# Layer 1's mask: turned 32 by 32 on VectorE, spread over rows by one 512-column product, with degrees summed by runs

## The chip, the cores and the metric

The kernel runs on one core of one Trainium2 chip. The metric is the device time of one execution in microseconds (us). Five engines work side by side, each through its own queue in order: TensorE (PE, with the loads of its stationary operand shown apart as PEld), VectorE (DVE), ScalarE (ACT), GpSimd (POOL) and SyncE (SP), which here only issues DMA transfers. They wait for one another through semaphores.

## The reference, cut to what matters

Two layers work on 128 graphs of 128 nodes with 256 features. Layer 0 (layernorm, a convolution, message passing, a gated update) fills most of the time and is not changed. Layer 1 runs a two-layer graph convolution on five groups of the first 25 nodes and adds the fused result:

```python
GROUPS = [list(range(25)), [0..8], [0, 9..14], [6, 7, 8, 12, 13, 14], [3, 4, 5, 9, 10, 11]]
A = adj + jnp.eye(n)                       # of one group: adj_g = adj[:, idx][:, :, idx]
deg = jnp.sum(A, axis=-1)
dinv = jnp.where(deg == 0, 0.0, deg_safe ** (-0.5))
norm_adj = dinv[:, :, None] * A * dinv[:, None, :]
out = relu(einsum(norm_adj, x @ W) + b)    # twice, W1 then W2
fused = fused.at[:, idx, :].add(norm_w[g] * out_g)
```

What changes is how `norm_adj` is built. For each group it is the group's part of the adjacency matrix plus the identity, scaled by the inverse roots of the row sums.

## The kernel before

**Tiling of layer 1.** The groups together have 25 + 9 + 7 + 6 + 6 = 53 rows (`NR`), padded to `RP = 64`. Two graphs share the 128 partitions, `s * 64 + r` being row r of graph s. A block is 16 graphs (`SB`), so 8 pairs; there are 8 blocks. Each group's node list is cut into runs of consecutive nodes by `_runs()`: 1 + 1 + 2 + 2 + 2 = 8 runs (row offset r, first node n, width w).

**Constants.** `_constants()` builds one array that is loaded in two parts. Of its columns `et` (node n to row k of both halves), `same` (rows of one group), `diag`, `e4`, `ones2`, `sgrp` (which group a row belongs to, per half) and `ident` matter here.

**`prepare(blk)`, lines 1015 to 1079,** makes the scaled masks `ac` and the copies `r4` of one block, in steps parted by `yield`:
1. L1023: SP issues four loads of the 25x25 corners of 16 adjacency matrices into `aj`, nodes on 25 partitions, 16 graphs along the free axis.
2. L1029: POOL adds the identity and copies the 8 runs' columns into `b1`, 25 partitions by 16 graphs by 64 rows.
3. L1036: DVE sums `b1` by group into `dg`, 5 reductions.
4. L1042: PE makes `pa`, eight products, one for each pair: `b1` of the pair (128 columns) is stationary, `et` (64 columns) moves. L1044: DVE multiplies by `same` into `ac`. L1047: PE spreads `dg` over rows (`et` stationary, 80 columns move). L1050 to L1059: DVE and POOL pick the row's group and form the inverse root `dm`.
5. L1063 to L1065: DVE scales; L1068: PE; L1069: DVE; L1073: PE makes `pr4` (512 columns); L1077: DVE copies it to `r4`.

`block(blk)` then uses `ac` and `r4`: products `py` (L1093), the five groups' two layers in `first` (L1110) and `second` (L1119), then `turn`, `gather` and `fuse`.

**What sets the order.** All engines' programs are written out by a list scheduler, `Order.run`, at build time. Each part of the work is a generator; `yield cost, delay` says how much PE time the step just issued takes, and how long its next step should wait. Lanes share PE by weight. In the last call the lane `second` holds `setup_1` and then `prepare` and `block` of each block in turn, two of them open at once, at weight 0.2, beside layer 0's groups (`stage_c`), its loads, `fetch` and `rows`. Costs and delays change the order of all engines' instructions, but no instruction waits for a time: at run time an engine stops only at semaphores. `block(blk)` starts when `prepare(blk)` has ended and block `blk - 1` has passed its `gather` steps; `prepare(blk)` starts after `prepare(blk - 1)`. In layer 0's last stage the DMA issues on POOL (L837, L938, L954, L955) and the powers on POOL (L1007) stand in the same queue as `prepare`'s adds.

**Buffers.** `aj` and `dd` share one buffer (tag `dd`); `b1` is set to zero once in `setup_1`.

Of the kernel before, what the change touches and what calls it, by code (L numbers as in the profile page):

```python
# [9 lines left out]
FP = mybir.dt.float32  # L10
AF = mybir.ActivationFunctionType
ALU = mybir.AluOpType
# [7 lines left out]
P = 128  # L20
GB = 4
# [9 lines left out]
SB = 16  # L31
# [4 lines left out]
NG = len(GROUPS)  # L36
# [8 lines left out]
def _runs():  # L45

    out = []
    for g, nodes in enumerate(GROUPS):
        i = 0
        while i < len(nodes):  # L50
            j = i
            while j + 1 < len(nodes) and nodes[j + 1] == nodes[j] + 1:
                j += 1
            out.append((OFFS[g] + i, nodes[i], j - i + 1))
            i = j + 1
    return out
# [36 lines left out]
def _constants():  # L93

    row_node = [n for g in GROUPS for n in g]
    row_group = [i for i, g in enumerate(GROUPS) for _ in g]
    fwd, inv, tap = _fourier()
    parts = {
        "ident": np.eye(P),
        "mhalf": np.full((P, 8), -0.5),  # L100
        "fwd": fwd, "tap": tap, "inv": inv,
        "ones2": np.kron(np.eye(2), np.ones((RP, RP))),
        "et": np.zeros((P, 2 * RP)),
        "same": np.zeros((P, RP)),
        "diag": np.zeros((P, RP)),
        "e4": np.zeros((P, P)),
        "s2": np.zeros((P, 2 * WIDE)),
        "grp": np.zeros((P, NG)),
        "sgrp": np.zeros((P, 2 * NG)),
        "grpt": np.zeros((P, P)),  # L110
        "sel": np.zeros((P, P)),
        "emb": np.zeros((P, 12)),
    }

    roles = {0: [(2, 2, 0), (0, 0, 1), (1, 1, 0), (0, 0, 1)],
             1: [(0, 0, -1), (0, 0, 1), (1, 1, 0), (1, 1, 0)],
             2: [(1, 1, 0), (1, 1, 0), (0, 0, -1), (0, 0, 1)]}
    for j in range(GB):
        for role, factors in roles.items():
            for ch in range(3):  # L120
                k = WIDE * j + 3 * role + ch
                parts["sel"][ch, k] = 1
                parts["emb"][k] = np.array(factors).T.reshape(-1)
    for r, (n, g) in enumerate(zip(row_node, row_group)):
        for s in range(2):
            k = s * RP + r
            parts["et"][n, k] = 1
            parts["same"][k, [i for i in range(NR) if row_group[i] == g]] = 1
            parts["diag"][k, r] = 1
            for j in (2 * s, 2 * s + 1):  # L130
                parts["e4"][k, j * WIDE + n] = 1
            parts["s2"][k, s * WIDE + n] = 1
            parts["grp"][k, g] = 1
            parts["sgrp"][k, s * NG + g] = 1
            parts["grpt"][g, k] = 1
    at, o = {}, 0
    for name, a in parts.items():
        at[name] = (o, o + a.shape[1])
        o += a.shape[1]
    return np.concatenate(list(parts.values()), 1).astype(np.float32), at  # L140
# [67 lines left out]
def kernel(ctx: ExitStack, tc: tile.TileContext, x, adj, consts, vecs, w_se, conv1_w,  # L208
# [25 lines left out]
    def c(name):  # L234
        a, b = CAT[name]
        return cst[:, a:b]
# [725 lines left out]
    def setup_1():  # L962
        while len(E_DONE) < NQ:
            yield 0.0, 1.0
        near.close()
        pool = S["pool"] = ctx.enter_context(
            tc.tile_pool(name="l1", bufs=1, reuse_waits="tile"))
        S["pool2"] = ctx.enter_context(
            tc.tile_pool(name="l2", bufs=2, reuse_waits="tile"))
        b2s = pool.tile([NG, D], FP, tag="dd", name="b2s")  # L970
        nc.sync.dma_start(out=b2s, in_=b2)
        for n in range(2):
            load_w1(n)
        S["w2"] = weight(pool, W2, [P, 5, 4, D], "g (k p) o -> p g k o", "w2", nc.sync)
        S["ac"] = [pool.tile([P, SB // 2, RP], FP, name=f"ac{i}") for i in range(2)]
        r4 = S["r4"] = [pool.tile([P, QS, GB, NR], FP, name=f"r4{i}") for i in range(2)]
        S["yz"] = pool.tile([P, 2, SB, RP], FP, name="yz")
        S["b1"] = pool.tile([NN, SB, RP], FP, name="b1")
        for t in (*r4, S["yz"][:, 0], S["yz"][:, 1], S["b1"]):
            nc.gpsimd.memset(t, 0.0)  # L980
            yield 0.0, 4.0
        b2row = S["b2row"] = pool.tile([P, D], FP, name="b2row")
        pb2 = ptmp.tile([P, 512], FP, tag="tmp", name="pb2")
        nc.tensor.matmul(pb2[:, :D], c("grpt")[:NG], b2s, start=True, stop=True)
        nc.vector.tensor_copy(b2row, pb2[:, :D])
        P_DONE.add(-1)
        B1_DONE.add(-1)
        yield 0.5, 0.0
# [26 lines left out]
    def prepare(blk):  # L1015

        while not (blk - 1 in P_DONE and blk - 2 in {-2, *B1_DONE}):
            yield 0.0, 1.0
        pool, pool2, b1 = S["pool"], S["pool2"], S["b1"]
        ac, r4 = S["ac"][blk % 2], S["r4"][blk % 2]  # L1020
        aj = pool.tile([NN, SB, NN], FP, tag="dd", name=f"aj{blk}")
        for i in range(GB):
            nc.sync.dma_start(out=aj[:, i % 2 * 2 + i // 2::GB],  # L1023
                              in_=adj[blk * SB + i:(blk + 1) * SB:GB, :NN, :NN]
                              .rearrange("b n m -> n b m"))
        yield 0.0, 13.0 if blk < NBLK - 1 else 6.0

        for r, n, w in _runs():
            nc.gpsimd.tensor_tensor(b1[:, :, r:r + w], aj[:, :, n:n + w],  # L1029
                                    ident[:NN, None, n:n + w].to_broadcast([NN, SB, w]),  # L1030
                                    ALU.add)
        yield 0.0, 5.0

        dg = pool2.tile([NN, SB, NG], FP, tag="dg", name=f"dg{blk}")
        for g in range(NG):
            nc.vector.reduce_sum(dg[:, :, g], b1[:, :, OFFS[g]:OFFS[g] + SIZES[g]],  # L1036
                                 axis=mybir.AxisListType.X)
        yield 0.0, 7.0

        pa = ptmp.tile([P, SB // 2, RP], FP, tag="tmp", name=f"pa{blk}")  # L1040
        for p in range(SB // 2):
            nc.tensor.matmul(pa[:, p], b1[:, 2 * p:2 * p + 2, :].rearrange("n s r -> n (s r)"),  # L1042
                             c("et")[:NN, :RP], start=True, stop=True)
        nc.vector.tensor_mul(ac, pa, c("same")[:, None, :].to_broadcast([P, SB // 2, RP]))  # L1044

        pdg = ptmp.tile([P, SB // 2, 2, NG], FP, tag="tmp", name=f"pdg{blk}")
        nc.tensor.matmul(pdg.rearrange("p a s g -> p (a s g)"), c("et")[:NN],  # L1047
                         dg.rearrange("n b g -> n (b g)"), start=True, stop=True)
        dsel = pool.tile([P, SB // 2, 2 * NG], FP, tag="dsel", name=f"dsel{blk}")
        nc.vector.tensor_mul(dsel, pdg.rearrange("p a s g -> p a (s g)"),  # L1050
                             c("sgrp")[:, None, :].to_broadcast([P, SB // 2, 2 * NG]))
        dm = pool.tile([P, SB // 2], FP, tag="dm", name=f"dm{blk}")
        zo = pool.tile([P, SB // 2], FP, tag="zo", name=f"zo{blk}")
        nc.vector.reduce_sum(dm, dsel, axis=mybir.AxisListType.X)
        nc.vector.tensor_scalar(zo, dm, 0.0, None, op0=ALU.is_equal)
        nc.vector.tensor_add(dm, zo, dm)
        nc.gpsimd.tensor_tensor(dm, dm, c("mhalf"), ALU.pow)
        nc.gpsimd.tensor_mul(zo, zo, dm)
        nc.gpsimd.tensor_sub(dm, dm, zo)  # L1059
        yield 2.0, 7.0  # L1060

        dd = pool.tile([P, SB // 2, RP], FP, tag="dd", name=f"dd{blk}")
        nc.vector.tensor_mul(dd, c("diag")[:, None, :].to_broadcast([P, SB // 2, RP]),  # L1063
                             dm[:, :, None].to_broadcast([P, SB // 2, RP]))
        nc.vector.tensor_mul(ac, ac, dm[:, :, None].to_broadcast([P, SB // 2, RP]))  # L1065
        yield 0.0, 6.0
        pg = ptmp.tile([P, SB // 2, RP], FP, tag="tmp", name=f"pg{blk}")
        nc.tensor.matmul(pg, c("ones2"), dd, start=True, stop=True)  # L1068
        nc.vector.tensor_mul(ac, ac, pg)  # L1069
        yield 0.9, 3.0  # L1070

        pr4 = ptmp.tile([P, QS, 2, RP], FP, tag="tmp", name=f"pr4{blk}")
        nc.tensor.matmul(pr4.rearrange("p q a r -> p (q a) r"), c("e4"), ac,  # L1073
                         start=True, stop=True)
        for j in range(GB):
            s = slice(j * WIDE, (j + 1) * WIDE)
            nc.vector.tensor_copy(r4[s, :, j % 2 * 2 + j // 2, :], pr4[s, :, j % 2, :NR])  # L1077
        yield 0.9, 1.0
        P_DONE.add(blk)
# [174 lines left out]
```

## Time and profile before

| | |
|---|---|
| median of 3 runs | 2012.26 us (2009.02 to 2017.96) |
| the profiled execution | 2009.44 us |
| its span on the core | 2007.7 us |
| PE busy | 1960.1 us (98%), 12598 matmul records |
| DVE busy | 1352.3 us (67%) |
| ACT, POOL busy | 683.4 us (34%), 655.7 us (33%) |
| L1042, the eight products, all blocks | 128 records, 15.9 us busy |
| L1029, the adds on POOL | 64 instructions, 27.7 us busy |
| L1036, the reductions on DVE | 40 instructions, 10.1 us busy |

An fp32 product shows as two records. A record's busy time includes its passage through the pipeline and overlaps the next one's; how long a product holds PE is read from one start to the next. In rows of groups the columns are line, engine, operation, output and inputs, shapes, count, then busy time and mean duration in ns, then the engine's idle time just before and what ended it.

### The profile page before, as it was taken

How to read it: one execution, taken by the hardware profiler on the slowest of the kernel's cores; microseconds unless marked ns; L12 is line 12 of the kernel's file. 1: busy time of each engine (PE TensorE's matmuls, PEld its weight loads, DVE VectorE, ACT ScalarE, POOL GpSimd, SP SyncE). 2: the span in 40 equal slices, each digit the busy share in tenths (PEclk: the TensorE clock that was granted, in tenths of full speed). 3: DMA queues.
4: the chain of work that ended last, by engine and by line, in shares of the span. 5: the costliest groups of instructions: out<-in, count | busy, mean ns of one | idle time of the engine just before them, and what ended most of it. 6: DMA issues, size and time to landing. Idle time of an engine off the chain costs nothing.

```text
span 2007.7 us, 33356 instructions
## 1 busy us (share of the span) xinstructions
PE 1960.1 (98%) x12598; PEld 1625.4 (81%) x12598; DVE 1352.3 (67%) x3002; ACT 683.4 (34%) x1547; POOL 655.7 (33%) x897
## 2 busy tenths in 40 slices
PE   7999999999999999999999999999999999999998
PEld 5667888889888888878778878888888888888865
DVE  6775445885433576885885787778668867886652
ACT  4664222454222344222323232232323332322233
POOL 3452666332656111241331232222221322222320
PEclk9999999999999999999999999999999999999999
DMA  9997879744887743542433342443442433433331
GB/s 212 296 273 250 274 250 289 220 148 158 269 258 254 198 124 107 163 103 82 119 90 108 106 113 77 118 112 88 118 121 80 126 102 98 107 102 108 65 94 53
DMA packets 184106, 302.88 MB, mean 151 GB/s; under 512 B 28501, under 2 KB 131994, under 8 KB 183690
## 3 DMA queue, kind: packets, MB, share of 16 engines
q1 hardware_dynamic: 138762, 168.81, 28.9%
q0 software_dynamic: 44800, 131.66, 22.6%
q8 instruction: 100, 1.64, 0.3%
q14 instruction: 60, 0.49, 0.1%
q10 hardware_dynamic: 384, 0.28, 0.1%
HBM read 204.12 MB, written 109.05 MB: 156 GB/s over the span
## 4 chain that ended last, share of the span: by engine, by line
PE 87%; DVE 7%; DMA 3%; issue 1%; ACT 1%; SPq 1%; POOL 0%; DVEq 0%; ACTq 0%; POOLq 0%
PE p L755 41%; PE pa L531 7%; PE ph L1110 5%; PE pz L1119 5%; PE pm L642 5%; PE pc L422 4%; PE pb L531 3%; PE px L668 3%; PE pf L433 3%; PE pi L712 3%; PE pw L477 1%; PE py L1093 1%; PE ph L411 1%; DMA xa<-in_x 1%; PE pse L626 1%
## 5 line engine op out<-in xcount | busy, mean ns | idle before, releaser
L938 POOL DMA_DIRECT2D x1d<-xt x128 | 101.1, 815 | 467.2 <-DVE xt L936 454.9
L837 POOL DMA_DIRECT2D xt<-in_x x128 | 100.2, 789 | 173.8 <-DMA x1d<-xt 166.8
L563 DVE SCALAR_TENSOR_TENSOR y<-pa,kk 128x512 f32<-128x512 f32 x78 | 53.8, 690 | 151.2 <-ACT kk L562 151.1
L531 PE MATMUL pa<-wf,X 128*128 128x256 f32 x640 | 152.2, 381 | 0.0
L755 PE MATMUL p<-th,wrz 128*128 128x256 f32 x512 | 134.5, 385 | 0.0
L755 PE MATMUL p<-tc,wrz 128*128 128x256 f32 x512 | 131.4, 379 | 0.0
L755 PE MATMUL p<-tm,wrz 128*128 128x256 f32 x512 | 131.4, 379 | 0.0
L531 PEld LDWEIGHTS pa<-wf,X 128*128 128x128 f32 x640 | 118.1, 190 | 16.2 <-issue 2.0
L422 PE MATMUL pc<-c1w,hTa 128*128 128x256 f32 x512 | 121.2, 383 | 2.7 <-DVE X L439 1.5
L642 PE MATMUL pm<-wmsg,hT 128*128 128x256 f32 x512 | 121.5, 382 | 0.0
L1110 PE MATMUL ph<-yz,w 128*128 128x96 f32 (+3 forms) x640 | 109.3, 325 | 1.4 <-DVE yz L1095 1.4
L422 PEld LDWEIGHTS pc<-c1w,hTa 128*128 128x128 f32 x512 | 94.0, 191 | 19.9 <-DVE h L425 4.8
L755 PEld LDWEIGHTS p<-th,wrz 128*128 128x128 f32 x512 | 94.7, 190 | 19.1 <-issue 7.3
L1112 ACT ACTIVATE hh<-ph,vec 128x96 f32<-128x96 f32 (+3 forms) x160 | 63.6, 401 | 133.5 <-PE ph L1110 125.1
L724 ACT ACTIVATE xc<-xc,t_bn 128x256 f32<-128x256 f32 x128 | 58.2, 500 | 148.5 <-DVE xc L721 148.5
L755 PEld LDWEIGHTS p<-tc,wrz 128*128 128x128 f32 x512 | 97.3, 190 | 13.9 <-issue 0.8
L642 PEld LDWEIGHTS pm<-wmsg,hT 128*128 128x128 f32 x512 | 95.8, 190 | 15.2 <-ACT kk L562 1.4
L1119 PE MATMUL pz<-hh,w 128*128 128x96 f32 (+3 forms) x640 | 107.5, 322 | 0.7 <-DVE yz L1121 0.7
L755 PEld LDWEIGHTS p<-tm,wrz 128*128 128x128 f32 x512 | 97.3, 190 | 13.2
L1110 PEld LDWEIGHTS ph<-yz,w 128*128 128x128 f32 x640 | 88.3, 193 | 22.4 <-issue 15.6
L1119 PEld LDWEIGHTS pz<-hh,w 128*128 128x128 f32 x640 | 86.3, 191 | 18.6 <-DVE yz L1121 1.3
L755 PE MATMUL p<-hTc,wrz 128*128 128x256 f32 x384 | 99.3, 381 | 1.2 <-DVE z L829 1.2
(204 smaller groups left out, 4464.8 us busy)
## 6 DMA issues: line engine op xcount, KB each, us to landing
wf<-wfd SPq DMA_DIRECT2D x160, 256.0 KB
wfd<-ws POOLq DMA_DIRECT2D x64, 320.0 KB, 10.2
yd<-y POOLq DMA_DIRECT2D x80, 256.0 KB, 4.0
yt<-yd SPq DMA_DIRECT2D x64, 320.0 KB
w<-in_W SPq DMA_DIRECT2D x40, 512.0 KB
xa<-in_x SPq DMA_DIRECT2D x128, 128.0 KB
hTd<-hTa POOLq DMA_DIRECT2D x32, 512.0 KB, 6.6
hT<-hTd SPq DMA_DIRECT2D x32, 512.0 KB
```

Of the source, the lines that this page charges most:

```text
L422: nc.tensor.matmul(pc[:, i], hT[:, k, (2 * h + i) * N:(2 * h + i + 1) * N], c1w[:, k], start=(k == 0), stop=(k == 1))
L433: nc.tensor.matmul(pf[:, i, :F * NB], h1[:, 2 * h + i, k * P:(k + 1) * P], fwd, start=True, stop=True)
L531: nc.tensor.matmul(ps, xk(k), WF[f][:, k, s], start=(k == 0), stop=(k == 1))
L642: nc.tensor.matmul(pm[:, i], hT[:, k, j * N:(j + 1) * N], LATE["wmsg"][:, k], start=(k == 0), stop=(k == 1))
L668: nc.tensor.matmul(px[:, dc, i], msgs[h][:, i, dc * P:(dc + 1) * P], aT[:, 2 * h + i], start=True, stop=True)
L712: nc.tensor.matmul(pi[w * WIDE:(w + 1) * WIDE, :, :, n].rearrange("p k g c -> p g k c"), inv[:F, o:o + WIDE], yt[:, n // 2::2].rearrange(" ...
L755: nc.tensor.matmul(ps[:, m], w[:, i, k, m * P:(m + 1) * P], factor(i, x, t), start=first and j == 0, stop=last and j == len(n) - 1, skip_g ...
L837: nc.gpsimd.dma_start(out=xt[a * WIDE:(a + 1) * WIDE].rearrange("p b d c -> p (b d) c"), in_=slices(x[q * GB:(q + 1) * GB])[a])
L938: nc.gpsimd.dma_start(out=slices(x1d[q])[a], in_=xt[a * WIDE:(a + 1) * WIDE].rearrange("p b d c -> p (b d) c"))
L1110: nc.tensor.matmul(ph, w1[:, k, m * P:(m + 1) * P], yz[:, k, :, o:o + n], start=(k == 0), stop=(k == 1))
L1112: nc.scalar.activation(hh[:, m], ph, AF.Relu, bias=v("b1", g * 4 + m))
L1119: nc.tensor.matmul(pz, w2[:, g, m, cc * P:(cc + 1) * P], hs[g][:, m], start=(m == 0), stop=(m == 3))
```

## The change

The load puts the two graphs of a pair on two blocks of 32 partitions (`s * 32 + n`), 8 pairs along the free axis, each padded to 32 columns; `aj` has a buffer of its own, set to zero once in `setup_1`. DVE transposes `aj` in 32x32 blocks into `at`, 64x256. POOL adds the identity (a new constant, `eye`) and copies the 8 runs from `at` into `b1`, now 64 partitions by 8 pairs by 64 rows. DVE sums `aj`, without the identity, by run into `dg`, 8 reductions, and 1 is added to the degree later. One product replaces the eight: `et`, now with 64 rows, is stationary, and all of `b1` (512 columns) moves. The degree product moves 64 columns in place of 80. Adds and reductions stand in one step with a delay of 9.0 in place of two with 5.0 and 7.0; the PE cost of the next step is 1.1 in place of 2.0. `setup_1` has one more memset.

```diff
@@ constants
-        "sgrp": np.zeros((P, 2 * NG)),
+        "sgrp": np.zeros((P, len(_runs()))),
+        "eye": np.zeros((P, WIDE)),
...
-            parts["et"][n, k] = 1
+            parts["et"][s * WIDE + n, k] = 1
+            parts["eye"][s * WIDE + n, n] = 1
...
-            parts["sgrp"][k, s * NG + g] = 1
+            parts["sgrp"][k, [i for i, (o, _, _) in enumerate(_runs())
+                              if OFFS[g] <= o < OFFS[g] + SIZES[g]]] = 1
@@ setup_1
-        S["b1"] = pool.tile([NN, SB, RP], FP, name="b1")
-        for t in (*r4, S["yz"][:, 0], S["yz"][:, 1], S["b1"]):
+        S["b1"] = pool.tile([2 * WIDE, SB // 2, RP], FP, name="b1")
+        S["aj"] = pool.tile([2 * WIDE, SB // 2, WIDE], FP, name="aj")
+        for t in (*r4, S["yz"][:, 0], S["yz"][:, 1], S["b1"], S["aj"]):
             nc.gpsimd.memset(t, 0.0)
             yield 0.0, 4.0
@@ prepare
-        aj = pool.tile([NN, SB, NN], FP, tag="dd", name=f"aj{blk}")
+        aj = S["aj"]
         for i in range(GB):
-            nc.sync.dma_start(out=aj[:, i % 2 * 2 + i // 2::GB],
+            s = i // 2 * WIDE
+            nc.sync.dma_start(out=aj[s:s + NN, i % 2::2, :NN],
                               in_=adj[blk * SB + i:(blk + 1) * SB:GB, :NN, :NN]
                               .rearrange("b n m -> n b m"))
         yield 0.0, 13.0 if blk < NBLK - 1 else 6.0
 
-        for r, n, w in _runs():
-            nc.gpsimd.tensor_tensor(b1[:, :, r:r + w], aj[:, :, n:n + w],
-                                    ident[:NN, None, n:n + w].to_broadcast([NN, SB, w]),
-                                    ALU.add)
-        yield 0.0, 5.0
-
-        dg = pool2.tile([NN, SB, NG], FP, tag="dg", name=f"dg{blk}")
-        for g in range(NG):
-            nc.vector.reduce_sum(dg[:, :, g], b1[:, :, OFFS[g]:OFFS[g] + SIZES[g]],
-                                 axis=mybir.AxisListType.X)
-        yield 0.0, 7.0
+        at = pool.tile([2 * WIDE, SB // 2, WIDE], FP, tag="dd", name=f"at{blk}")
+        nc.vector.transpose(at.rearrange("p a n -> p (a n)"), aj.rearrange("p a n -> p (a n)"))
+        dg = pool2.tile([2 * WIDE, SB // 2, len(_runs())], FP, tag="dg", name=f"dg{blk}")
+        for i, (r, n, w) in enumerate(_runs()):
+            nc.gpsimd.tensor_tensor(b1[:, :, r:r + w], at[:, :, n:n + w],
+                                    c("eye")[:2 * WIDE, None, n:n + w]
+                                    .to_broadcast([2 * WIDE, SB // 2, w]), ALU.add)
+            nc.vector.reduce_sum(dg[:, :, i], aj[:, :, n:n + w], axis=mybir.AxisListType.X)
+        yield 0.0, 9.0
 
-        for p in range(SB // 2):
-            nc.tensor.matmul(pa[:, p], b1[:, 2 * p:2 * p + 2, :].rearrange("n s r -> n (s r)"),
-                             c("et")[:NN, :RP], start=True, stop=True)
+        nc.tensor.matmul(pa, c("et")[:2 * WIDE], b1, start=True, stop=True)
...
-        pdg = ptmp.tile([P, SB // 2, 2, NG], FP, tag="tmp", name=f"pdg{blk}")
-        nc.tensor.matmul(pdg.rearrange("p a s g -> p (a s g)"), c("et")[:NN],
-                         dg.rearrange("n b g -> n (b g)"), start=True, stop=True)
+        pdg = ptmp.tile([P, SB // 2, len(_runs())], FP, tag="tmp", name=f"pdg{blk}")
+        nc.tensor.matmul(pdg, c("et")[:2 * WIDE], dg, start=True, stop=True)
...
         nc.vector.reduce_sum(dm, dsel, axis=mybir.AxisListType.X)
+        nc.vector.tensor_scalar(dm, dm, 1.0, None, op0=ALU.add)
...
-        yield 2.0, 7.0
+        yield 1.1, 7.0
```

More of the change, by code (lines that the diff above doesn't have):

```diff
@@ L1047, in prepare @@
-        nc.tensor.matmul(pdg.rearrange("p a s g -> p (a s g)"), c("et")[:NN],
-                         dg.rearrange("n b g -> n (b g)"), start=True, stop=True)
-        dsel = pool.tile([P, SB // 2, 2 * NG], FP, tag="dsel", name=f"dsel{blk}")
-        nc.vector.tensor_mul(dsel, pdg.rearrange("p a s g -> p a (s g)"),
-                             c("sgrp")[:, None, :].to_broadcast([P, SB // 2, 2 * NG]))
+        pdg = ptmp.tile([P, SB // 2, len(_runs())], FP, tag="tmp", name=f"pdg{blk}")
+        nc.tensor.matmul(pdg, c("et")[:2 * WIDE], dg, start=True, stop=True)
@@ L1052, in prepare @@
+        dsel = pool.tile([P, SB // 2, len(_runs())], FP, tag="dsel", name=f"dsel{blk}")
+        nc.vector.tensor_mul(dsel, pdg, c("sgrp")[:, None, :].to_broadcast(
+            [P, SB // 2, len(_runs())]))
         dm = pool.tile([P, SB // 2], FP, tag="dm", name=f"dm{blk}")
```

## The prediction

> **What bounds the kernel now.** I read the page's busy times first, then the busy times by stage, then the one row of timeline where the changed lines run, and last the waits of TensorE (PE).
>
> ```profile
> PE 1960.1 (98%) x12598; PEld 1625.4 (81%) x12598; DVE 1352.3 (67%) x3002; ACT 683.4 (34%) x1547; POOL 655.7 (33%) x897
> ...
> PE 87%; DVE 7%; DMA 3%; issue 1%; ACT 1%; SPq 1%; POOL 0%; DVEq 0%; ACTq 0%; POOLq 0%
> ```
>
> PE is busy 98% of the span and carries 87% of the chain that ended last. Busy shares of a pipelined PE are generous, so I look at the stages in which the changed code runs: PE has instructions of layer 1 from 838 us on. In each row the columns are stretch, its length, and busy time (with instructions) of PE, weight loads, DVE, ACT, POOL.
>
> ```profile
> 838.00:900.00 62.00, 59.96 (x377) 49.60 (x377) 53.60 (x117) 16.53 (x35) 22.04 (x33) 0.97 0.36 89
> 1000.00:1200.00 200.00, 196.64 (x1253) 163.17 (x1252) 150.67 (x325) 56.96 (x126) 54.26 (x76) 1.00 0.38 104
> 1400.00:1600.00 200.00, 200.00 (x1327) 166.40 (x1326) 154.89 (x331) 59.70 (x130) 53.72 (x77) 1.00 0.39 108
> 1916.00:2008.00 92.00, 78.21 (x516) 57.50 (x516) 36.49 (x94) 29.47 (x68) 15.58 (x26) 0.98 0.27 74
> ```
>
> Seven of the eight `prepare` calls end their PE work inside 838 to 1916, where PE is full and DVE has a quarter free; the eighth falls in the tail, where 13.8 us of PE are idle. In a full stage PE time removed is time gained, one for one, and other engines' work is free as long as it is not late. The row of the timeline around the first call (start, length, engine):
>
> ```profile
> 871.24 0.59 PE L755 MATMUL p<-xc,wn 128*128 128x256 f32 x2
> 871.76 1.99 PE L1042 MATMUL pa<-cst,b 25*128 25x64 f32 x16
> 873.60 0.40 PE L1047 MATMUL pdg<-dg,cst 25*128 25x80 f32 x2
> 873.92 1.23 PE L755 MATMUL p<-hTc,wrz 128*128 128x256 f32 x4
> ```
>
> Lengths overlap (a matmul's end is modelled), so I use starts. An fp32 product is two records: 8 products of 64 columns are 16 records and hold PE from 871.76 to 873.60, 1.84 us; the degree product holds it to 873.92, 0.32 us. The starts in the trace give 1.83 and 0.33 us in all eight blocks. What a 512-column product holds PE for stands in the same trace, twice per block:
>
> ```profile
> 1905.80 1.02 PE L1068 MATMUL pg<-dd,cst 128*128 128x512 f32 x2
> 1906.66 0.59 PE L755 MATMUL p<-xm,wn 128*128 128x256 f32 x2
> ```
>
> That is 0.86 us, the figure of 12 of the 16 products L1068 and L1073; two have 0.96 and two, in the tail, 1.06.
>
> **What the Trainium skill says.** "TensorE: Matmul & The Clock Gate", LDWEIGHTS: a load takes its stationary columns / 1.2 in ns, whatever the rows, so 106.7 ns for 128 columns. The trace agrees: 16 records in 1.83 us are 114 ns each, although only 64 columns move. So the old form pays for sixteen weight loads and not for its columns, and 64 instead of 25 stationary rows should cost nothing. The same page, Back-to-back issue gap, calls a wide matmul bound by its moving columns; here the two records of 512 fp32 columns took 0.86 us, twice the 0.43 of the two of 256 just ahead of them (1905.37 to 1905.80). "VectorE: DVE Perf Modes", errata section, prices an fp32 tensor_tensor at (N+151)/0.96 ns. The trace is near it for the reductions too: 400 elements took 551 ns (574 by the formula). "GPSIMD Engine Reference", Performance versus the Vector engine: about 2.6 cycles per element for two inputs. The trace agrees: from the groups below 2.0 ns per element (2.4 cycles at the page's 1.2 GHz) plus 238 ns an instruction, and 743 ns for 256 elements in 128 partitions (L525; 745 by that line), so partitions are free and only the elements in each count.
>
> The groups of adds and reductions, kept apart by shape (busy us, mean ns):
>
> ```profile
> L1029 POOL TENSOR_TENSOR b<-aj,cst 25x400 f32<-25x400 f32 x8 | 8.3, 1032 | 0.1
> L1029 POOL TENSOR_TENSOR b<-aj,cst 25x16 f32<-25x16 f32 x8 | 2.2, 270 | 0.0
> ...
> L1036 DVE TENSOR_REDUCE dg<-b 25x16 f32<-25x400 f32 x8 | 4.4, 551 | 0.0
> L1036 DVE TENSOR_REDUCE dg<-b 25x16 f32<-25x96 f32 x16 | 3.2, 236 | 0.0
> ```
>
> **The change part by part,** per `prepare` call, eight of them.
>
> *PE.* Removed: the eight products, 1.83 us. Added: one product of 512 columns, 0.86 us. The degree product goes from 80 to 64 moving columns and from 25 to 64 rows; it is two loads of 128 columns either way, so 0.33 us stays. Net 1.83 - 0.86 = 0.97 us, times 8 = 7.8 us. With the slower 0.96 it is 7.0; if the degree product's first load now hides under the 512 columns (one load, 0.11 us, saved) it is 8.6.
>
> *POOL.* Before, 8 adds over 16 graphs: 8 x 238 ns + 16 x 53 elements x 2.0 ns = 3.6 us. After, 8 adds over 8 slots, 424 elements: 1.9 + 0.8 = 2.7 us. POOL is freed by 0.9 us. But its first add now waits for the DVE transpose; behind it on POOL stand the DMA issues of L837, L938, L954/955 and the powers of L1007.
>
> *DVE.* Five reductions over 848 elements become eight over 424. By their groups 137 ns + 1.04 ns per element, so 1.57 us before and 1.54 after. Added: one `tensor_scalar` of 8 elements (0.17, as L1055) and the transpose of 64x256. No row shows that size; a 128x512 transpose took 709 ns (L719) and 1052 with a permuting pattern (L929), so half, 0.35 to 0.53 us; I take 0.4. Together +0.55 us. Against this DVE's idle time for `pa` shrinks: it stood 1.50 us ahead of 873.79 until the eighth product was out, and should stand some 1.0 us less. DVE is not the bound (about 151 of 200 us busy), so nothing reaches the end. With its cover gone, 0.55 x 8 = 4.4 us is the most.
>
> *The DMA.* Four loads as before, 400 packets of 100 bytes, to other partitions. They now meet DVE, not POOL, first. In the trace the packets of every block are over within 6.4 us of the first issue, and the adds, whose step the transpose takes, start 14 to 49 us after the last issue. So no wait. `aj` no longer shares a buffer with `dd`; only its own old readers hold it, long done. The late constants grow by 30 columns, 15 KB on 461.5, under layer 0; the extra memset (64x256; 25x1024 took 0.97 us) is some 0.25 us of POOL, once.
>
> *The order.* One pause of 9 us replaces 5 and 7, the PE cost goes from 2.0 to 1.1, and the setup has one more memset with a pause of 4 us. The first block's chain starts 4 us later and is 3 + 0.9 us shorter: nothing, under a PE busy 59.96 of 62 us. From then on the list scheduler picks other interleavings. Where PE is at 200 of 200 us there is little to win; between 900 and 1916 it idles 5.4 us in all.
>
> *The tail.* Here the chain of `prepare(7)` is exposed:
>
> ```profile
> 1961.06 1.12 PE L1073 MATMUL pr<-ac,cst 128*128 128x512 f32 x2
> 1962.11 0.65 PE L1163 MATMUL pfu<-zt,s2w 128*64 128x256 f32 x4
> 1963.91 3.10 PE L1093 MATMUL py<-r,x1h 128*128 128x212 f32 x16 [1.15 <-DVE r L1077]
> ```
>
> Block 7's first product waits 1.15 us for the copies of the last step of `prepare(7)`. `prepare`'s product stands after the third `second` of block 6; with 9 for 5 + 7 it comes one or two steps of 1.95 us earlier, and so does all behind it: 2 to 4 us, more than the 1.15 and the 0.17 ahead of `pg`. I count 1.3 us, with bounds 0 and 3.
>
> Sum: 7.8 + 1.3 = 9.1 us. The profiled execution took 2009.44 us (span 2007.7, 1.7 around it): 2000.3. The median of the runs, 2012.26, lies 2.8 above that execution, so on the median **2003**.
>
> **The rivals.**
>
> *A better order.* The new order also fills PE gaps that the change does not touch: 5.4 us between 900 and 1916, 2.0 between 838 and 900, 3.7 in the waits from 1916 to 1926. Half of these is some 6 us: 15 us in all, 1997. For it: the rows show the gaps. Against: nothing in the change aims at them.
>
> *The gain is eaten.* The 512-column product exposes its first load and a wait (1.06 as in the tail, 0.3 of issue more), or the order opens gaps as it closes others. Gain 0.97 - 0.5 = 0.5 per block and nothing in the tail: 4 us, 2008. For it: PE's weight loads of L755 already stand 20.3 us in gaps put down to issue from 838 us on.
>
> *Late masks, slower.* Before, the DMA, POOL and DVE took turns with 5 + 7 us between them; now DMA, DVE, POOL, PE have 9. The chain needs 0.4 (transpose) + 2.7 (adds) = 3.1 us, a little more with its semaphores, and the reductions run beside it. It decides when DVE lags PE's place in the order by over some 6 us: every microsecond more stops PE in each block. A lag of 9 us costs 3 x 8 = 24 us, less the 9.1: about 2027. Against: DVE used PE's results within 1 to 2 us around 852 to 872 (L882 at 871.87, right behind its product at 871.24), and the adds started 12.8 to 46 us ahead of PE's product in all blocks, so some 10 us with the pause cut by 3.
>
> **How the numbers follow.** A change of 0.5%, 10 us, is about what a measurement of this kernel can tell from none; runs of the same kernel spread by 9 us. Likeliest case 0.56 (2000 to 2007), better order 0.20, eaten 0.14, late 0.10. The bound of 0.5% faster is 2002.2. Of the likeliest case I put a bit under four tenths below it, with all of the better order: 0.22 + 0.20 = 0.42 faster. The rest of it and the eaten case: 0.34 + 0.14 = 0.48 same. Late: 0.10 slower. The range takes in the eaten case down to no gain at all, and leaves out the late case and the far end of the better order: 1995 to 2012.
>
> **What would show it.** Right: two records at the new product with 0.86 us to the next start, no PE wait at it; DVE waits under 1 us for `pa`; eight adds in about 2.7 us; PE busy time down by 7 to 9 us; no wait of `py` for the copies of L1077's successor in the tail. Wrong: DVE idle before the transpose with the DMA as releaser, PE idle before the new product with POOL as releaser, or new PE waits at L755.

## The result and the profile after

The changed kernel took 1999.99 us (median of 6 runs, 1997.61 to 2005.25), the kernel before 2012.4 in the same comparison: ratio 0.9935, 95% interval 0.9914 to 0.9955. Two more comparisons of the same pair gave 0.9952 (0.9926 to 0.9977) and 0.9917 (0.9893 to 0.9940). The forecast was 2003 with 1995 to 2012. The kernel before, run against itself, came out at 0.9987 (0.9975 to 1.0000), so some 3 us of such a ratio can come from the comparison alone.

The profiled execution took 1999.49 us, its span 1997.7, 10.0 less than before. From the page, busy time by engine:

```profile
PE 1950.6 (98%) x12486; PEld 1610.6 (81%) x12486; DVE 1349.5 (68%) x3042; ACT 683.2 (34%) x1547; POOL 650.1 (33%) x898
```

PE is down by 9.5 us and still the bound; no other engine grew. The row of the timeline around the first call of `prepare`:

```profile
870.56 1.03 PE L758 MATMUL p<-xc,wrz 128*128 128x256 f32 x4
871.52 1.12 PE L1044 MATMUL pa<-b,cst 64*128 64x512 f32 x2
872.48 0.33 PE L1048 MATMUL pdg<-dg,cst 64*128 64x64 f32 x2
872.74 1.13 PE L758 MATMUL p<-th,wrz 128*128 128x256 f32 x4
```

The wide product holds PE from 871.52 to 872.48, 0.96 us, and the degree product to 872.74, 0.26 us. The starts give 0.96 and 0.26 in all eight blocks: 1.22 us where the old pair held PE 2.16.

The groups of the new steps from 838 us on, by shape (busy us, mean ns, idle before them and what ended it):

```profile
L1037 POOL TENSOR_TENSOR b<-at,cst 64x24 f32<-64x24 f32 x32 | 7.3, 253 | 0.0
L1045 DVE TENSOR_TENSOR ac<-pa,cst 128x512 f32<-128x512 f32 x8 | 5.5, 692 | 6.0 <-PE pa L1044 6.0
L1037 POOL TENSOR_TENSOR b<-at,cst 64x200 f32<-64x200 f32 x8 | 4.5, 562 | 21.2 <-DVE at L1034 18.5 <-PE ph L1111 2.6
L1034 DVE STREAM_TRANSPOSE at<-aj 64x256 f32<-64x256 f32 x8 | 3.4, 424 | 0.0
L1040 DVE TENSOR_REDUCE dg<-aj 64x8 f32<-64x24 f32 x32 | 3.4, 163 | 0.0
```

The transpose takes 0.42 us and waits for no DMA. POOL waits for it (18.5 us in all), and nobody waits for POOL. DVE's wait for `pa` is 6.0 us in 8 calls, 0.75 each, where before it was 9.3 in 6 of the 8:

```profile
L1044 DVE TENSOR_TENSOR ac<-pa,cst 128x512 f32<-128x512 f32 x8 | 5.5, 691 | 9.3 <-PE pa L1042 9.3
```

### The profile page after: what moved, and what is told of

Its sections match the earlier page's. It is cut to its first block, busy times and chain, and to the rows that moved or that the text cites. A ratio compares the mean times of both kernels' runs of the same rounds, so it can differ in the third digit from the quotient of the medians.

```text
span 1997.7 us, 33167 instructions
## 1 busy us (share of the span) xinstructions
PE 1950.6 (98%) x12486; PEld 1610.6 (81%) x12486; DVE 1349.5 (68%) x3042; ACT 683.2 (34%) x1547; POOL 650.1 (33%) x898
## 4 chain that ended last, share of the span: by engine, by line
PE 86%; DVE 6%; DMA 4%; issue 1%; ACT 1%; POOL 1%; SPq 0%; DVEq 0%; POOLq 0%; ACTq 0%
PE p L758 40%; PE pa L534 7%; PE ph L1111 5%; PE pm L645 5%; PE pz L1120 5%; PE pc L425 4%; PE pb L534 3%; PE pf L436 3%; PE px L671 3%; PE pi L715 2%; PE pw L480 1%; PE ph L414 1%; PE py L1094 1%; PE pg L1154 1%; PE pse L629 1%
```

## The experiments

Three readings are used. The timed ratio to the kernel before has an interval of some 2 to 5 us on either side. A profile can be read finer if the part ahead of the change is left out: up to 178 us, where the DMA engines are busy 90% of the time or more, the profiles differ by up to 8.5 us, whatever the kernel. So "body" below is the time from a fixed PE product at 692 us (the second group's first `pi` product) to the end of the span. In it the granted clock fell to half in stretches of 3.41 us or a multiple; each such stretch costs half its length, 1.7 us, and the last column takes that out. (A fall that every profile has in its last 3 to 6 us is not counted; PE has no product left there.)

| kernel, one profile each | body, us | clock falls in it | less the falls |
|---|---|---|---|
| before | 1315.45 | 2 | 1312.0 |
| before, second profile | 1316.78 | 3 | 1311.7 |
| before, more constants | 1316.38 | 2 | 1313.0 |
| new order, eight products | 1314.71 | 1 | 1313.0 |
| before, wider small products | 1316.11 | 2 | 1312.7 |
| changed | 1310.27 | 1 | 1308.6 |
| changed, second profile | 1307.98 | 1 | 1306.3 |
| changed, third profile | 1308.12 | 1 | 1306.4 |
| changed, no setup pause | 1305.59 | 1 | 1303.9 |
| new data path, old order | 1305.28 | 1 | 1303.6 |
| the same, second profile | 1304.12 | 0 | 1304.1 |
| changed, product twice | 1314.81 | 1 | 1313.1 |

The third reading is of all executions that have a mean granted clock on record beside their time. A clock at half for some time loses half of that time, so span x (1 - granted clock) is the time lost in one execution. (This counts low clock where PE has nothing to do as well, such as the last 3 to 6 us, much alike in all kernels.) Among the executions of one kernel, 1 us more lost goes with 0.9 us more time. The means, in us, with the executions of one kernel put together:

| kernel | executions | time | granted clock | lost | time less the loss |
|---|---|---|---|---|---|
| before | 134 | 2013.1 | 0.9944 | 11.3 | 2001.8 |
| new order, eight products | 14 | 2012.4 | 0.9944 | 11.2 | 2001.2 |
| before, wider small products | 22 | 2010.3 | 0.9960 | 7.9 | 2002.3 |
| changed | 19 | 2001.2 | 0.9971 | 5.8 | 1995.4 |
| changed, no setup pause | 6 | 2000.5 | 0.9962 | 7.7 | 1992.8 |
| new data path, old order | 11 | 1997.5 | 0.9974 | 5.3 | 1992.3 |
| changed, product twice | 20 | 2008.6 | 0.9967 | 6.7 | 2001.8 |
| changed, short pause | 22 | 2009.7 | 0.9939 | 12.3 | 1997.3 |

The standard error of the last column is 0.2 to 0.6, and 0.9 with 6 executions. The mean of before is 11.9 us over that of the changed kernel: 5.5 us of it is clock and 6.4 us is not.

**The changed kernel again.** Of the 10.0 us between the first two profiles, 4.7 were there at 178 us, ahead of anything changed.

> The changed kernel once more, for a narrower interval. The two profiles differ by 10.0 us, of which 4.7 were there at 178 us, ahead of any instruction that the change touches. If that head start is chance, the change is worth the sum of the prediction, 7 to 9 us (ratio 0.9955 to 0.9965), and the head start varies from profile to profile. If it belongs to the change (30 more columns of constants), it comes back and the ratio stays near 0.9935.

Measured: ratio 0.9952 (0.9926 to 0.9977); the second profile reached the same product at 178.51 us, against 178.53 before and 173.83 in the first. The head start was chance.

**More constants alone.** 30 more columns, nothing else:

```diff
         "sgrp": np.zeros((P, 2 * NG)),
+        "pad": np.zeros((P, 30)),
```

> The kernel before with 30 more columns of constants and nothing else. If the head start of 4.7 us at 178 us is chance: the same as before, ratio 0.999 to 1.001. If it comes from the larger constants: 4 to 5 us faster, ratio 0.9977.

Measured: 0.9994 (0.9977 to 1.0012), body as before. The constants are worth nothing.

**The data path alone.** The pauses and costs of before, so that PE's order is that of before, with one product where eight stood:

```diff
                                     .to_broadcast([2 * WIDE, SB // 2, w]), ALU.add)
+        yield 0.0, 5.0
+        for i, (r, n, w) in enumerate(_runs()):
             nc.vector.reduce_sum(dg[:, :, i], aj[:, :, n:n + w], axis=mybir.AxisListType.X)
-        yield 0.0, 9.0
+        yield 0.0, 7.0
...
-        yield 1.1, 7.0
+        yield 2.0, 7.0
```

(The memset of `aj` goes into another's step, without a pause.)

> The new data path (transpose, one product, degrees by runs) under the pauses and costs of before: PE's order is that of before, one product in place of eight. Product theory: PE shortens by 0.94 us in each of 8 blocks, 7.5 us, ratio 0.9963, at once and evenly. Order theory (the new interleaving gives most of the gain): under 3 us, ratio above 0.9985. Late-mask rival: PE waits at the new product, which would show as idle time there.

Measured: 0.9924 (0.9902 to 0.9946). Here every PE product has its partner in the profile of before, so the two can be laid side by side. The lead is the time by which a product comes earlier than its partner. This is where it changed by more than 0.3 us from 838 us to the end:

```
before, us   step in the lead, us   place
 860.70          0.85               small waits
 865.05         -0.36               small waits
 873.60          0.87               after the product, block 0
 874.67-878.30   1.75               granted clock at half in before
 901.62         -0.77               wait for ve (1.13 here)
 921.30          0.94               pz waits 0.67 for yz in before
 930.53          0.87               block 1
1016.81          1.20               py waits 1.0 for x1h in before
1033.30          0.89               block 2
1269.86          0.73               block 3
1271.52-1274.57  1.71               granted clock at half in before
1500.98          0.88               block 4
1656.93          0.95               block 5
1869.21          0.94               block 6
1947.73          0.94               block 7
```

The eight products are there, one for one, 7.1 us together. Beside them stand two steps of 1.7 us that were not foreseen, and 1.9 us net of other waits.

**The order alone.** PE's order of the changed kernel, with 25 partitions, `b1` from `aj` without a transpose, the eight products and a degree product of 128 columns. Beside the changed kernel the main difference is:

```diff
-        nc.tensor.matmul(pa, c("et")[:2 * WIDE], b1, start=True, stop=True)
+        for p in range(SB // 2):
+            nc.tensor.matmul(pa[:, p], b1[:, 2 * p:2 * p + 2, :].rearrange("n s r -> n (s r)"),
+                             c("et")[:NN, :RP], start=True, stop=True)
```

> PE's order of the changed kernel, but with 25 partitions, no transpose and the eight products (degrees by runs, 128 columns). Product theory: within 2 us of before, ratio 0.999 to 1.001; what is left is the order, 0 to 1.3 us in the tail. Better-order rival: 4 to 6 us faster, ratio 0.997 to 0.998.

Measured: 0.9995 (0.9982 to 1.0009); the eight products and the degree product held PE 2.20 us. The better-order rival falls: with the eight products the new order gives nothing that can be measured, and the clock loses as much as before (11.2 us).

**Twice the product.**

```diff
-        nc.tensor.matmul(pa, c("et")[:2 * WIDE], b1, start=True, stop=True)
+        for _ in range(2):
+            nc.tensor.matmul(pa, c("et")[:2 * WIDE], b1, start=True, stop=True)
```

> The changed kernel with the 512-column product issued twice into the same tile. If PE's stream is the bound, one for one: 0.86 us more per block, 6.9 us slower than the changed kernel, ratio to before 0.997 to 0.998. If part of it hides: under 3 us.

Measured: 0.9972 (0.9957 to 0.9987), 0.0037 over the mean 0.9935 of the changed kernel's three ratios, so 7.4 us slower; by the body less the falls 1313.1 - 1307.1 = 6.0, by the executions less the loss 6.4. PE's timeline in block 3:

```profile
1240.72 1.98 PE L1045 MATMUL pa<-b,cst 64*128 64x512 f32 x4
1242.55 0.33 PE L1049 MATMUL pdg<-dg,cst 64*128 64x64 f32 x2
1242.80 0.70 PE L758 MATMUL p<-xm,wn 128*128 128x256 f32 x2
```

The pair holds PE 2.08 us, 0.86 more than 1.22. Eight times 0.86 is 6.9. PE time in these stages is paid in full, within these errors.

**The late masks.** The pause ahead of the product cut:

```diff
-        yield 0.0, 9.0
+        yield 0.0, 2.0
```

> The changed kernel with the pause ahead of the product cut from 9 to 2 us. In its profiles the adds end 4 to 10 us ahead of the product. Late-mask theory: with 7 us less the adds come too late in most blocks and PE idles 1 to 4 us at the product, 8 to 25 us slower than the changed kernel, ratio to before near 1.000 to 1.007. If the order still leaves the product behind enough PE work: no wait, the same as the changed kernel.

Measured: 0.9980 (0.9966 to 0.9993), 9 us slower than the changed kernel. The waits of PE from 700 us on (us in total, times, longest), and the third block in its timeline:

```profile
PE pa L1044 <- POOL b L1037: 8.4, 2, 5.0
```

```profile
991.76 1.95 PE L715 MATMUL pi<-yt,cst 80*32 80x128 f32 x64
998.74 2.07 PE L1044 MATMUL pa<-b,cst 64*128 64x512 f32 x2 [5.02 <-POOL b L1037]
1000.60 0.53 PE L1048 MATMUL pdg<-dg,cst 64*128 64x64 f32 x2
1001.06 2.07 PE L758 MATMUL p<-th,wrz 128*128 128x256 f32 x4
```

The late-mask chain exists, but in two blocks of eight: in the others 2 us of pause still left PE enough to do. What made the two dear is the row after the wait: 0.96 us of product became 1.86 (998.74 to 1000.60), because the granted clock was at half, for 10.24 us from 996.0. Waits of 8.4 us and clock falls of 6.83 and 10.24 us (8.5 us lost) go together. Over the executions 6.5 of the 8.5 us by which the mean is over the changed kernel's are clock (12.3 us lost against 5.8).

**The clock.** In the kernel before, the granted clock fell to half right behind some of the eight products. Stretches of 3.4 us before (first profile, block 0), before (second profile, block 1) and after (block 1); the third number from the right is the granted clock:

```profile
871.40:874.80 3.40, 3.40 (x24) 2.91 (x24) 1.40 (x4) 1.11 (x2) 0.00 (x0) 1.00 0.50 152
874.80:878.20 3.40, 3.40 (x10) 2.70 (x9) 3.19 (x12) 0.00 (x0) 2.65 (x4) 0.50 0.02 7
```

```profile
925.30:928.70 3.40, 3.40 (x30) 3.21 (x29) 0.83 (x3) 0.00 (x0) 0.00 (x0) 1.00 0.54 154
928.70:932.10 3.40, 3.40 (x17) 3.40 (x18) 1.13 (x5) 1.02 (x3) 1.87 (x3) 0.50 0.00 0
```

```profile
919.00:922.40 3.40, 3.40 (x23) 2.70 (x23) 1.86 (x7) 0.46 (x2) 0.00 (x0) 1.00 0.56 159
922.40:925.80 3.40, 3.40 (x33) 3.40 (x33) 0.86 (x4) 1.22 (x4) 2.06 (x3) 1.00 0.28 95
```

PE is "busy" 3.40 of 3.40 us ahead of each of these falls, so by the records it never paused. Over all profiles a fall began within 4 us of the eight products in 7 of 32 calls (2, 2, 2 and 1 of 8 in before, before again, more constants, new order) and of the one product in 0 of 56 (seven profiles; the kernels with the short pause and with weight 0.3, in which PE stood still, are left out, and so is the one with wider products).

Which calls are hit can be read from the times of the falls. In each profile all falls begin a whole number of 3.413 us apart: before has them at 171.68, 874.82, 1270.77 and 2004.63 us, 206, 116 and 215 such steps. Cut the profiles into windows by this grid. In 7 of the 32 calls the first of the eight products began within the first 1.12 us of a window, so that all eight and the degree product (2.16 us) lay whole in it, and at the end of that window the clock fell all 7 times. In the other 25 it began at 1.36 us or later, and no fall followed. The one product began within the first 1.12 us of a window in 14 of its 56 calls, and no fall followed. So where the windows happen to lie decides which calls are hit, and of the two forms only the eight products make a window that is answered by a fall. (This split was seen in the profiles afterwards and was not forecast.)

If the windows lie at random, a call is hit with a chance of 1.12 / 3.413 to 1.36 / 3.413; that is 2.6 to 3.2 falls in an execution of before, an estimate of 4.5 to 5.4 us from these figures, and the executions say 5.5. (The falls away from the products, at 779 to 787, 1049 to 1064 and 1918 us, come behind windows in which PE was busy for at most 2.52 of 3.41 us.)

To see whether the 64 moving columns are too little work for the clock, they were doubled. (Two PSUM tiles now hold the result, so DVE multiplies by `same` in two halves.)

```diff
-            nc.tensor.matmul(pa[:, p], b1[:, 2 * p:2 * p + 2, :].rearrange("n s r -> n (s r)"),
-                             c("et")[:NN, :RP], start=True, stop=True)
+            nc.tensor.matmul(pas[p // 4][:, p % 4],
+                             b1[:, 2 * p:2 * p + 2, :].rearrange("n s r -> n (s r)"),
+                             c("et")[:NN], start=True, stop=True)
```

> The kernel before, with the eight products moving 128 columns in place of 64 (the second half copies the first and is not used), in two PSUM tiles. PE's weight loads stay the bound, so each product should still hold PE some 0.23 us (16 records in 1.8 to 1.9 us). In the profiles so far the granted clock fell to half for 3.4 us next to the eight products in 2, 2 and 1 of 8 blocks (before, constants only, new order with eight products), and in none of 24 blocks with the one product. Theory that the 64-column products are too little work for the clock: no such fall here, 3.4 us faster than before, ratio 0.998 to 0.999. Rival (chance, or the loads themselves): falls of the clock next to these products remain, ratio 0.9995 to 1.001.

Measured: 0.9978 (0.9966 to 0.9991), which is the forecast of the theory. The eight products held PE 1.89 us, where with half the columns it was 1.84, so it is not the moving columns that hold PE. But the profile has a fall right behind the products of block 7, and one at 783 us away from any:

```profile
1943.80:1947.20 3.40, 3.40 (x30) 3.21 (x29) 1.77 (x7) 0.30 (x1) 1.75 (x3) 1.00 0.91 245
1947.20:1950.60 3.40, 3.40 (x19) 3.40 (x18) 0.10 (x2) 1.06 (x4) 2.54 (x4) 0.50 0.32 69
```

So wider products lessen the falls and do not end them: four of its calls began within the first 1.12 us of a window (0.10, 0.12, 0.53 and 0.80), and one of the four was hit instead of all. The executions agree. The clock loses 7.9 us instead of 11.3, and the time less the loss is that of before (2002.3 and 2001.8), so all of the gain is clock. That the falls go with the eight products and not with the one is shown by the counts and by the executions. That few moving columns in one window are too little work for the clock fits the wider products, but what the clock counts as work stays open.

**The kernel before, profiled again.**

> The kernel before as a kernel of its own, for a second profile. Ratio 0.999 to 1.001. If the eight products invite falls of the granted clock, at least one of its 8 blocks shows one within 4 us of them; if the five seen in 24 were chance, none may.

Measured: 0.9987 (0.9975 to 1.0000), with falls behind the products at 928.7 and 1270.0 us, as was forecast from the first profiles, and one at 1918.5 away from them.

**The old order again, and the setup pause.** The table has the changed kernel at 1306.3 to 1308.6 less the falls, the data path in the old order at 1303.6.

> The new data path in the old order, once more. In the first profile its time from a fixed product at 692 us to the end was 10.2 us under that of before, where the changed kernel had 5.2 and 7.5. If the old order is worth 3 us over the new one, this comes back: ratio 0.993 to 0.995, against 0.994 to 0.996 for the changed kernel. If not, 0.995 to 0.996.

Measured: 0.9907 (0.9884 to 0.9930), body 1304.1 less the falls. Then the changed kernel without the pause of 4 us that comes with the new memset:

```diff
-        for t in (*r4, S["yz"][:, 0], S["yz"][:, 1], S["b1"], S["aj"]):
+        nc.gpsimd.memset(S["aj"], 0.0)
+        for t in (*r4, S["yz"][:, 0], S["yz"][:, 1], S["b1"]):
             nc.gpsimd.memset(t, 0.0)
             yield 0.0, 4.0
```

> The changed kernel with the extra memset in the step of another, so without the 4 us pause that the change adds to the setup. Set side by side by PE's own order, the changed kernel and the new data path in the old order part between 841 and 926 us, by 2 to 3 us, and not after. If the pause does it (rows come later than block 0's masks; PE waited 2.0 us for x1h and 1.4 for ac): those waits go, 2 to 3 us faster than the changed kernel in the same call. If the shorter pause ahead of the product does it: no change, within 1 us.

> The changed kernel a third time, beside the two above on the same chip. Ratio to before 0.993 to 0.996; granted clock: no fall to half next to the one product in its 8 blocks.

Measured together: 0.9924 (0.9901 to 0.9948) without the pause, 0.9917 (0.9893 to 0.9940) with it. The ratios can't tell them apart. The profiles do: 1303.9 less the falls against 1306.4 in the third profile of the changed kernel. In block 0 of the changed kernel:

```profile
892.48 1.13 PE L1074 MATMUL pr<-ac,cst 128*128 128x512 f32 x2 [1.43 <-DVE ac L1070]
```

and in the old order, where the same product comes without a wait:

```profile
892.69 1.02 PE L1077 MATMUL pr<-ac,cst 128*128 128x512 f32 x2
```

Without the pause this wait is gone. So by the profiles the pause costs some 2.5 us. The executions less the loss agree: 1992.8 without it (standard error 0.9) and 1995.4 with it. The old order has 1992.3, so nothing that can be measured is left for the order itself. The new order with the eight products has the same pause and shows no loss by it (2001.2 against 2001.8 of before); there the wait is 0.3 us.

**A larger share for layer 1.** On top of the old order:

```diff
-              Lane(second, ahead=2, weight=0.2)
+              Lane(second, ahead=2, weight=0.3)
```

> The new data path in the old order with layer 1's lane at weight 0.3 in place of 0.2, to see whether it beats both kernels. Layer 1 then lags less and less of it is left behind layer 0's end, where PE idles some 7 us between 1906 us and its last product. If that idle time shrinks: 2 to 4 us faster than the old order at 0.2. If layer 0's groups are then left with too little beside them: the same or slower.

Measured: 1.0160 (1.0135 to 1.0185), 49 us slower than the old order at 0.2 by the mean of that one's two ratios (0.9916). Its waits of PE:

```profile
PE py L1097 <- ACT x1h L1016: 23.6, 13, 3.5
PE p L758 <- DVE r L880: 11.0, 17, 1.6
```

Layer 1 now overtakes the rows that it needs: `py` waits for them 13 times, 23.6 us. And `r`, the wait of layer 0's own chain, shows 11.0 us from 838 us on where before has 4.5. The clock fell to half six times ahead of the last one, for 30.7 us in all.

## Why the prediction was right

**Right.** The bound and the exchange: PE time removed in a full stage came back one for one (side by side, 0.73 to 0.95 us per block; twice the product, 0.86 per block, cost 6.0 to 7.4 us). The size of the exchange: 0.97 us a block forecast, 0.94 measured, 7.5 us in all in place of 7.8. It is made up otherwise than written: the wide product holds PE 0.96 and not 0.86 us, the slower value of the bounds, and the degree product 0.26 and not 0.33. DVE's transpose (0.42 us for 0.4), its wait for `pa` (0.75 us, forecast under 1), POOL's adds (2.4 us by the groups, forecast 2.7) and the absent DMA wait came as forecast, and none reached PE. The late-mask rival was placed rightly: in the changed kernel's first profile the adds end 4 to 11 us ahead of the product, and with 7 us less they come too late in two blocks.

**Wrong in size: the tail.** 1.3 us were counted for block 7's first product, which waited for the last copies of `prepare(7)`. That wait is gone, as forecast:

```profile
1948.91 0.65 PE L1164 MATMUL pfu<-zt,s2w 128*64 128x256 f32 x4
1949.49 1.27 PE L1154 MATMUL pg<-zt,ac 64*64 64x256 f32 x8
1950.69 0.98 PE L1094 MATMUL py<-r,x1h 128*128 128x212 f32 x4
1951.61 0.65 PE L1164 MATMUL pfu<-zt,s2w 128*64 128x256 f32 x4
1952.19 0.98 PE L1094 MATMUL py<-r,x1h 128*128 128x212 f32 x4
...
1956.68 7.62 PE L1111 MATMUL ph<-yz,w 128*128 128x400 f32 x32 [0.52 <-issue]
```

But from block 6's first `ph` to block 7's it is 41.85 us before and 40.85 after, 1.00 less, of which the product is 0.94: the tail gave 0.1. The two rows of before, and the first of after (the second stands above):

```profile
1925.64 7.65 PE L1110 MATMUL ph<-yz,w 128*128 128x400 f32 x32 [0.92 <-DVE yz L1095]
1967.49 7.65 PE L1110 MATMUL ph<-yz,w 128*128 128x400 f32 x32 [0.47 <-DVE yz L1095]
...
1915.83 7.65 PE L1111 MATMUL ph<-yz,w 128*128 128x400 f32 x32 [1.25 <-DVE yz L1096]
```

`py` now stands between the `fuse` products, 0.91 us each where four in a row took 3.10, and one `pg` group just ahead of it takes 1.20 instead of 0.59. The new order draws block 7's first products forward: the wait is gone, and the steps there follow worse on one another.

**Missing: the clock.** A term of its own was left out. The profiles show it too small: before has 2.3 falls of the granted clock in the body, on the mean of its three profiles (with more constants counted in), the changed kernel 1.0 in its three, so at 1.7 us each 2.3 us. By the counts of those behind the products alone it is 7/32 x 8 x 1.7 = 3.0 us. Over the executions it is 5.5 us, nearly as much as all the rest of the gain. The one fall that the changed kernel has in each profile lies at 779 to 787 us, in code that is not changed. The low clock of 0.97 in the row 838 to 900 stood among the lines shown, and was not followed.

**Missing: the setup pause.** "The first block's chain starts 4 us later and is 3 + 0.9 us shorter: nothing" failed: less the falls, the changed kernel's body gains 5.1 us, the data path in the old order, which has no such pause, 8.4 (1312.2 against 1307.1 and 1303.9), and over the executions less the loss the gains are 6.4 and 9.5 us.

**Luck.** The sum came near because the errors cancelled. The forecast was 9.1 us. The exchange gave 7.5 and the tail 0.1, the pause took some 2.6, and the clock, put at nothing, gave 5.5: 10.5 us, where the means differ by 11.9. The last 1.4 us are not placed. Without the clock the gain would have been some 6.4 us, still inside the range. The bodies of the profiles say 1316.2 - 1308.8 = 7.4 us and the timed ratios 10 to 17. Most of that gap is clock as well: the three profiled executions of before (one of them with more constants) had a granted clock of 0.995 to 0.997, where 0.9944 is the mean of all, so they lost 8.0 us on the mean, 3.3 less than the 11.3 of all, while those of the changed kernel lost 6.0, near its 5.8.

**The chances.** Same (0.48) stood a little over faster (0.42); the ratio 0.9935 is past the bound of 0.5%, its interval reaches to 0.9955, and the second comparison (0.9952) lies on the other side of the bound. The better-order rival's time of 1997 was near, but not for its reason.

## What to carry to other kernels

On a PE that is full, a group of products with few moving columns costs its weight loads (here 1.84 us with 64 columns each and 1.89 with 128): turn it so that the constant is stationary and the many columns move, and count starts, not busy times. When such a stage changes, look at the granted clock as well as at the waits, and take its mean over many executions: one profile shows only where the windows happened to lie. Pauses and costs in a scheduler are worth undoing one at a time: here one pause of 4 us in the setup took back some 2.5 us.

## What the runs showed of the hardware

- The granted clock fell to half in pieces of 3.41 us (or 6.83, 10.24), which in each profile begin on one grid of 3.413 us. It fell both behind real waits (5.02 us of idle PE) and behind windows that the records show as fully busy: at 874.8 us after sixteen 64-column records, 1.7 us lost.
- Such a group of sixteen records was followed by a fall in 7 of the 7 calls that began within the first 1.12 us of a window of this grid, and in none of the 25 others. With 128 moving columns it was 1 of 4 such calls, with one product of 512 columns 0 of 14.
- A product of 512 fp32 columns held PE 0.86 us in 12 of 16 calls of L1068 and L1073 in the kernel before, and 0.96 as `pa` in all eight, where it has 64 rows and mostly follows on products with 128; issued again behind itself it took 0.86 (1.82 for two). Whether the rows or the load that came first made the 0.10 us was not tried.
- An fp32 transpose of 64x256 on VectorE took 424 ns; adds on GpSimd over 64 partitions took 562 ns for 200 elements, 12% under what 238 ns and 2.0 ns per element, read from 25 partitions, give (638).
